# Time and band attention on one core: value banks, shared roots, score order, and 64-key halves for the band scores

## The chip, the cores and the metric

One core of one Trainium2 chip runs the whole program. The metric is device time in microseconds of one execution. The kernel before took 2722.84 us (median of three runs, 2720.51 to 2723.32).

## What is computed

The input is x of shape [2, 256, 128, 128] in fp32: 2 batches, 256 time steps, 128 frequency bins, 128 channels. Three blocks follow each other, each with a layer norm ahead and a residual around it: causal attention over time (4 heads of 32 channels), attention over frequency inside a band of 16 bins to both sides, and a feed-forward block of 512 inner channels with an exact gelu.

```python
xt = _ln(x, ln_t_w, ln_t_b).transpose(0, 2, 1, 3)
x = x + _mha(xt, t_wi, t_bi, t_wo, t_bo, H_T, cm).transpose(0, 2, 1, 3)   # cm: causal
xf = _ln(x, ln_f_w, ln_f_b)
x = x + _mha(xf, f_wi, f_bi, f_wo, f_bo, H_F, bm)                         # bm: |i - j| <= 16
xn = _ln(x, ln_n_w, ln_n_b)
h = jax.nn.gelu(xn @ w1.T + b1, approximate=False)
x = x + (h @ w2.T + b2)
```

## The kernel before

**Groups.** The work is cut into groups of 512 rows of 128 channels (NT = 4 tiles of 128 rows). First come 128 `OverTime` groups: two frequency bins with all 256 time steps each. Then come 16 runs; a run is 8 `OverBands` groups (four time steps with all 128 bins each), followed by 8 `FeedForward` groups on the same rows. The time stage writes its result to DRAM, from where the runs load it.

**One group's way.** VectorE takes mean and variance (`statistics`, L447). The reciprocal root of the variance comes from a pair of ScalarE functions, Ln and Exp (`root_by_scalar`, L462), and three small VectorE steps (`refine`, L474), for the time groups with a PSUM bank as intermediate place (`root_in_bank`, L470). `normalize` (L483) writes the normalized rows, `turn` (L500) transposes them in blocks of 32 and sends them to DRAM, and `fetch` (L512) brings them back with channels on the partitions. TensorE makes queries and keys (`queries_keys`, L576) and values (`values`, L595); ScalarE copies all three from PSUM to SBUF (`take_query`, `take_key`, and `take_values`, L602). TensorE makes the scores, ScalarE their exponentials, GpSimd masks them; `weigh` sums the weights by a product with ones (into `rp`) and weighs the values (into `op`); ScalarE and VectorE invert the sums and divide (`invert`, L607; `divide`, L620: `bank<-bank,r`, then `u`, then `oT`); TensorE makes the output product and VectorE adds it to the residual (`finish`, L641).

**Matmuls by tiles.** All products use a part of the TensorE array. Products with a weight of 32 columns work in tiles of 128 rows by 32 columns. Scores have only 32 channels of a head to sum over: head h lies in row group h. With 64 keys such a product takes one of eight tiles of 32 rows by 64 columns: the row group is the head, the column group the 64-key half. With 128 keys it takes one of four tiles of 32 by 128. In fp32 each product is two passes, and the trace counts each pass.

**Scores over time.** For one group and head there are 8 products with 64 keys each. They are named by kind, head, sequence s and half e, as in `f110`: kind f (`first_scores`, L678) are the keys of the first 128 steps against all later queries (256 queries for half 0, 192 for half 1), kind s (`second_scores`, L685) the keys of the second 128 steps (64 queries for half 0, 128 for half 1). One block holds the s products of group n and the f products of group n+1, 32 in all, in an order written out by hand (`TIME_ORDER`, L738; `time_scores`, L744).

**Scores over bands.** `OverBands.scores` (L764) goes over four tiles of 128 bins. Tiles 0 and 3 are cut in halves of 64 keys, each with the 80 queries that the band reaches; tiles 1 and 2 take 128 keys and 128 queries at once. Head 3's band is applied by VectorE (`bank<-bank,band`), the other three are masked by GpSimd after the exponentials.

**Order of the work.** `run` (L1057) is one loop over n, in which each step of a group is written at the iteration and place where it is to be issued. Every instruction goes through `InOrder.pinned` (L881), which keeps that program order on each engine; so the profile shows L881 for all of them, and groups are told apart by the names of their tiles.

**Banks.** PSUM has eight banks. In the time stage they have names: a0 to a3 take the f scores of heads 0 to 3, b0 to b3 the s scores; `Attention.place` gives the other results a bank that is free at that moment, and after each iteration the names move round in a cycle (end of `run`). In the bands banks are taken in turn. A bank is taken again only after its reader is done; this makes the waits between engines.

**Input.** `load` (inside `groups`, L956 and L988) issues the DMAs for x, twelve groups ahead in the steady state, into a ring of four tiles of four groups each. The very first tile is `k.x0`, loaded at the start.

Of the kernel before, what the change touches and what calls it, by code (L numbers as in the profile page):

```python
# [19 lines left out]
P = 128  # L20
H = 4
D = 32
BAND = 16
# [404 lines left out]
class Group:  # L428
# [17 lines left out]

    def statistics(self):  # L447
        path, vector = self.path, self.path.vector
        self.mv = path.small.tile([P, NT, 2], F32, name="mv", bufs=16)
        stats = path.small.tile([P, NT, 6], F32, name="stats")  # L450
        for i in range(NT):
            vector.bn_stats(stats[:, i, :], self.src()[:, i, :])
        for i in range(NT):
            vector.bn_aggr(self.mv[:, i, :], stats[:, i, :])

    def root(self):
        path, gpsimd = self.path, self.path.gpsimd
# [3 lines left out]

    def root_by_scalar(self, to=None):  # L462

        path = self.path
        ln = path.small.tile([P, NT], F32, name="lnv")
        path.scalar.activation(ln, self.mv[:, :, 1], AF.Ln, bias=path.eps)
        self.root0 = path.small.tile([P, NT], F32, name="root0") if to is None else to
        path.scalar.activation(self.root0, ln, AF.Exp, scale=-0.5)

    def root_in_bank(self):  # L470
        path = self.path
        self.root_by_scalar(path.ps[path.banks["b2"]][:, 0:NT])

    def refine(self):  # L474

        path, vector, y = self.path, self.path.vector, self.root0
        t = path.small.tile([P, NT], F32, name="vy")
        vector.scalar_tensor_tensor(t, self.mv[:, :, 1], EPS, y, ALU.add, ALU.mult)
        vector.scalar_tensor_tensor(t, t, -0.5, y, ALU.mult, ALU.mult)
        self.rstd = path.small.tile([P, NT], F32, name="rstd", bufs=16)  # L480
        vector.scalar_tensor_tensor(self.rstd, t, 1.5, y, ALU.add, ALU.mult)

    def normalize(self):  # L483
# [60 lines left out]
    def values(self):  # L544
        pass
# [17 lines left out]
        pass  # L563


class Attention(Group):
    which = None
    swapped = ()
    place = {}
# [88 lines left out]
class OverTime(Attention):  # L658
# [4 lines left out]
    swapped = (1, 3)  # L663
    early, late = (1, 2), (0, 3)

    def first_tiles(self):
        path = self.path

        self.p0 = path.work.tile([P, 2, H, 2 * P], F32, name="p0", tag="p", bufs=3)
        self.s0 = {h: path.bank([P, 2, 2 * P], "sp", path.banks[f"a{h}"]) for h in range(H)}  # L670
# [65 lines left out]


TIME_ORDER = """  # L738
    s000 s301 s011 s300 f101 f211 s100 s311 s010 s001 s111 f300 f110 f000 f210 f301
    f201 f011 f200 f111 s310 f100 f010 f310 s211 f311 s201 f001 s110 s101 s210 s200  # L740
""".split()


# [14 lines left out]
class OverBands(Attention):  # L758
# [5 lines left out]
    def scores(self, heads):  # L764
        path = self.path
        self.sp = {h: path.bank([P, NT * P], "sp") for h in heads}
        for i, part in ((0, HALF), (1, P), (2, P), (3, HALF)):
            reach = 0 if part == P else BAND
            for e in range(0, P, part):
                a = i * P + (e - reach if e else 0)  # L770
                q, keys = slice(a, a + part + reach), slice(i * P + e, i * P + e + part)
                for h in heads:
                    r = rows_of(h)
                    path.tensor.matmul(
                        self.sp[h][e : e + part, q], self.kT[r, keys], self.qT[r, q], start=True, stop=True
                    )

    def first_function(self):
# [107 lines left out]
class BoundedPath:  # L886
    def __init__(self, ctx, tc, k):
        self.tc, self.nc, self.k = tc, tc.nc, k
        self.xpool = ctx.enter_context(tc.tile_pool(name="xpool", bufs=3))
        self.work = ctx.enter_context(tc.tile_pool(name="work", bufs=3))  # L890
        self.small = ctx.enter_context(tc.tile_pool(name="small", bufs=6))
        ps = ctx.enter_context(tc.tile_pool(name="ps", bufs=1, space=PSUM))
        self.ps = [ps.tile([P, BANK], F32, name=f"bank{i}", tag=f"bank{i}") for i in range(8)]
        self.next_bank = 0
        self.held = {}
        self.banks = dict(zip(("a1", "a2", "b0", "b3", "a0", "a3", "b1", "b2"), range(8)))
        self.tensor, self.vector = InOrder(tc, tc.nc.tensor), InOrder(tc, tc.nc.vector)
        self.scalar, self.gpsimd = InOrder(tc, tc.nc.scalar), InOrder(tc, tc.nc.gpsimd)
        self.sync = InOrder(tc, tc.nc.sync)
        self.dram = ctx.enter_context(tc.tile_pool(name="turns", bufs=3, space=DRAM))  # L900
        self.zero = 0.0
        self.once = once = ctx.enter_context(tc.tile_pool(name="once", bufs=1))
        self.eps = once.tile([P, 1], F32, name="eps")
        tc.nc.vector.memset(self.eps, EPS)

        self.band = once.tile([P, P], F32, name="band")
        tc.nc.gpsimd.memset(self.band, 0.0)
        for s in (1, -1):
            tc.nc.gpsimd.affine_select(
                out=self.band, in_=self.band, compare_op=ALU.is_ge, fill=-1e30, base=BAND,  # L910
                pattern=[[-s, P]], channel_multiplier=s,
            )
# [25 lines left out]
    def quad(self, held, name, bufs):  # L938

        held[name] = self.xpool.tile([P, NT, NT, P], F32, name=name, tag=name, bufs=bufs)  # L940

    @staticmethod
    def longer(quad, i, a):

        return quad.rearrange("p s t c -> p (s t c)")[:, i * P - a : (i + 1) * P + D - a]

    def groups(self, x, out):
# [3 lines left out]
        for b in range(B):  # L951
            for f0 in range(0, FB, GA):
                held = {}


                def load(g, f0=f0, b=b, held=held):  # L956
                    if b == f0 == 0:
                        held["x"] = k.x0
                        return
                    if g == 0:  # L960
                        self.quad(held, "x", 4)
                    f = f0 + g // NC_T * NT
                    self.sync.dma_start(held["x"][rows_of(g)], self.of_times(x[b], g, slice(f, f + NT)))

                def store(g, f0=f0, b=b, held=held):
                    for i in range(NT if g % 2 else 0):
                        f = f0 + i // NC_T * NT + g
                        self.sync.dma_start(
                            self.of_times(k.x1[b], i, slice(f - 1, f + 1)), held["res"][rows_of(i), :, g - 1 : g + 1]
                        )  # L970

                def part(name, g, i=None, a=0, held=held):
                    if name == "res" and name not in held:
                        self.quad(held, "res", 2)
                    if i is not None:
                        return self.longer(held[name], i * NT + g, a)
                    return held[name][:, :, g]

                for g in range(NT):
                    yield OverTime(self, partial(part, "x", g), partial(part, "res", g), partial(load, g), partial(store, g))  # L980
        for b in range(B):
            for r0 in range(0, T, RUN):
                run = []
                for t0 in range(r0, r0 + RUN, GB):
# [2 lines left out]

                    def load(g, t0=t0, b=b, held=held):  # L988
                        if g == 0:
                            self.quad(held, "x", 4)  # L990
                            self.quad(held, "x2", 2 * RUN // GB)
                        self.sync.dma_start(
                            held["x"][rows_of(g)].rearrange("q g t c -> q (g t) c"),
                            self.of_bands(k.x1[b], t0 + NT * g, NT),
                        )
# [61 lines left out]
    def run(self, x, out):  # L1057
# [12 lines left out]
                do(n, *names)  # L1070


        run0 = [i for i in range(len(groups)) if at(i, OverBands)][: RUN // NT]
        due = dict(zip(run0, (-5, -4, -4, -3, -1, 0, 1, 2)))
        due = {n: [i for i in run0 if run0[0] + due[i] == n] for n in range(-12, len(groups) + 2)}
# [3 lines left out]
        for n in range(-12, len(groups) + 2):  # L1079
# [6 lines left out]
            do_at(n + 4, FeedForward, "root")  # L1086
            do(n, "first_half", "first_function", "first_mask")
            if n >= 0:
                do_at(n + 5, OverTime, "statistics")
            if old is not None or new is not None:  # L1090
                time_scores(old, new)
                b = self.banks
                Attention.place = dict(yp=b["b0"], rp=b["b3"], op=b["a1"], qp=b["a2"], kp=b["b1"], vp=b["b2"])
            else:
                Attention.place = {}
            if old is not None:
# [9 lines left out]
            if new is not None:  # L1106
                new.first_weights(new.early[1:])
            if n >= 0:
                do_at(n + 5, OverTime, "root_in_bank")
            if turn:  # L1110
                do(n, "second_half", "second_function")
            do_at(n + 3, OverTime, "fetch")
            do_at(n + 2, (OverBands, FeedForward), "fetch")

            for i in (2 * n + 12, 2 * n + 13) if n < -2 else (n + 10,) if n < 2 else ():
                if i >= NT:
                    do(i, "load")
            if n < -8 or n >= 0:
                do(n + 12, "load")
            if n >= 0:  # L1120
                for i in due[n]:
# [4 lines left out]
                do(n - 2, "finish")  # L1126
            do_at(n + 4, OverTime, "turn")
            if n >= 0:
                do_at(n + 5, OverTime, "refine")
            if n < 0:  # L1130
                do(n + 5, "statistics")
            do_at(n + 5, FeedForward, "statistics")
# [34 lines left out]
            if old is not None or new is not None:  # L1167

                b = self.banks
                self.banks = dict(  # L1170
                    a1=b["b1"], a2=b["a2"], b0=b["a0"], b3=b["a3"], a0=b["b0"], a3=b["b3"], b1=b["a1"], b2=b["b2"]
                )


# [67 lines left out]
```

## Time and profile before

| | |
|---|---|
| time, median of three runs | 2722.84 us (2720.51 to 2723.32) |
| profiled execution | 2717.44 us |
| its span, first to last instruction | 2715.7 us |
| mean granted TensorE clock | 0.998 |
| busy: TensorE / its weight loads | 2687.0 / 1817.2 us |
| busy: VectorE / ScalarE / GpSimd | 2181.6 / 1854.8 / 1947.9 us |
| DMA, mean | 128 GB/s |

In lines of the profile, PE is TensorE's matmuls, PEld its weight loads, DVE VectorE, ACT ScalarE, POOL GpSimd, SP the engine whose queue issues the DMAs. A line of a timeline has the start in us from the start of the span, the length, the engine, the line of code, the operation, out<-in by tile names, partitions by elements, and xN for N instructions of the same kind in a row; brackets give idle time ahead of it and what ended it. In a block of matmuls, the length shown goes to the modelled end of the last one, and the next block may begin before that. PSUM tiles are all called `bank`. Names that help: `qT,kT` are score products, `xnT,wf` queries and keys, `wf,xnT` values, `p,ones` and `p,v` (bands: `pf`) the weighing, `wn,oT` the output product, `xnT,w1f` and `w2T_sb,hT` the feed-forward products.

### The profile page before, as it was taken

What the parts mean: (1) busy time and instruction counts of PE and PEld (TensorE: products, weight loads), DVE (VectorE), ACT (ScalarE), POOL (GpSimd) and SP (SyncE); (2) the same over time, 40 slices, a digit from 0 to 9 for tenths busy, and PEclk for the clock granted to TensorE, in tenths of its full rate; (3) what the DMA queues carried; (4) which work ended last, traced back from release to release, by engine and by line L of the source; (5) the groups of instructions that cost most, each with busy time, mean ns of one, the idle gap of its engine ahead of it and who ended that gap; (6) DMA issues with size and microseconds to landing.
All of it is one profiled execution on the core that took longest, in us unless ns stands there. A gap on an engine that the chain in (4) does not pass through costs nothing.

```text
span 2715.7 us, 152631 instructions
## 1 busy us (share of the span) xinstructions
PE 2687.0 (99%) x66614; PEld 1817.2 (67%) x66614; DVE 2181.6 (80%) x6708; ACT 1854.8 (68%) x3620; POOL 1947.9 (72%) x2297
## 2 busy tenths in 40 slices
PE   8999999999999999999999999999999999999998
PEld 5676776767676666666666666666666666666665
DVE  6888888888888896977868769678687696886874
ACT  6999999999999864564655746646556466465563
POOL 4999999999999885756667657566666575665762
PEclk9999999999999999999999999999999999999999
DMA  5555555555555444445445454454444444544533
GB/s 148 146 152 153 150 150 149 150 147 147 147 159 148 131 113 121 117 112 129 111 117 133 105 125 122 112 131 107 118 129 110 124 118 113 131 108 119 131 92 82
DMA packets 471496, 346.83 MB, mean 128 GB/s; under 512 B 43296, under 2 KB 405152, under 8 KB 470816
## 3 DMA queue, kind: packets, MB, share of 16 engines
q1 hardware_dynamic: 469568, 335.92, 47.2%
q8 instruction: 524, 8.59, 1.4%
q10 hardware_dynamic: 1248, 1.05, 0.2%
q14 instruction: 156, 1.28, 0.2%
HBM read 169.03 MB, written 167.77 MB: 124 GB/s over the span
## 4 chain that ended last, share of the span: by engine, by line
PE 86%; DVE 11%; DMA 1%; issue 0%; ACT 0%; POOL 0%; SPq 0%; DVEq 0%; POOLq 0%; ACTq 0%
PE bank L881 86%; DVE xh L881 2%; DVE bank L881 2%; DVE stats L881 1%; DVE u L881 1%; DVE z L881 1%; DVE x L881 1%; DVE oT L881 1%; DMA xnT<-turned 1%; DVE mv L881 1%; DMA x<-in_x 0%; POOL p L881 0%; POOL pf L881 0%; DMA rows_sb<-in_rows 0%; DMA turned<-z 0%
## 5 line engine op out<-in xcount | busy, mean ns | idle before, releaser
L881 ACT ACTIVATE hT<-bank,b 128x512 f32<-128x512 f32 x512 | 346.7, 687 | 527.3 <-PE bank L881 508.5
L881 POOL TENSOR_SCALAR_AFFINE_SELECT pf<-pf 128x512 f32<-128x512 f32 x768 | 476.8, 635 | 291.0 <-ACT pf L881 264.5
L881 DVE TENSOR_SCALAR xh<-x,mv,rstd 128x160 f32<-128x160 f32 x1536 | 597.0, 431 | 14.3
L881 PEld LDWEIGHTS bank<-w2T_sb,hT 128*32 128x32 f32 x16384 | 457.1, 110 | 63.2 <-issue 39.7
L881 PE MATMUL bank<-xnT,wf 128*32 128x512 f32 x4096 | 488.6, 594 | 3.0 <-ACT p L881 3.0
L881 PE MATMUL bank<-w2T_sb,hT 128*32 128x128 f32 x16384 | 474.3, 273 | 0.2 <-ACT hT L881 0.2
L881 PE MATMUL bank<-xnT,w1f 128*32 128x512 f32 x4096 | 472.7, 592 | 0.0
L881 ACT ACTIVATE p<-bank 128x512 f32<-128x512 f32 (+1 forms) x1024 | 430.5, 495 | 30.6 <-PE bank L881 4.6
L881 POOL TENSOR_SCALAR_AFFINE_SELECT p<-p 128x1024 f32<-128x1024 f32 (+2 forms) x384 | 363.5, 947 | 92.6 <-ACT p L881 84.3
L881 DVE TENSOR_TENSOR res<-bank,res 128x512 f32<-128x512 f32 x256 | 175.8, 687 | 253.8 <-PE bank L881 250.5
L881 PE MATMUL bank<-qT,kT 32*64 32x80 f32 (+5 forms) x14336 | 368.2, 288 | 3.6 <-DVE oT L881 2.2
L881 PEld LDWEIGHTS bank<-qT,kT 32*64 32x64 f32 (+1 forms) x14336 | 300.5, 138 | 84.4 <-ACT kT L881 48.8
L881 PEld LDWEIGHTS bank<-wf,xnT 128*32 128x32 f32 x8192 | 233.1, 110 | 157.6 <-issue 102.8
L881 POOL TENSOR_TENSOR p<-p,p 128x512 f32<-128x512 f32 x256 | 324.1, 1288 | 10.7
L881 ACT ACTIVATE pf<-bank 128x512 f32<-128x512 f32 x512 | 264.5, 603 | 92.5 <-PE bank L881 92.0
L881 DVE BATCH_NORM_STATS2 stats<-x 128x6 f32<-128x128 f32 x1536 | 326.6, 275 | 0.1
L881 PEld LDWEIGHTS bank<-xnT,w1f 128*32 128x32 f32 x4096 | 150.5, 110 | 193.9 <-issue 169.0
L881 DVE STREAM_TRANSPOSE z<-xh 128x512 f32<-128x512 f32 x384 | 272.1, 709 | 9.3
L881 PE MATMUL bank<-wn,oT 128*32 128x128 f32 x8192 | 274.8, 274 | 0.4 <-ACT p L881 0.3
L881 POOL TENSOR_TENSOR rstd<-rstd,mhalf 128x4 f32<-128x4 f32 x248 | 256.6, 1035 | 20.7
L881 PE MATMUL bank<-wf,xnT 128*32 128x128 f32 x8192 | 271.1, 273 | 0.0
L881 POOL TENSOR_SCALAR rstd<-mv 128x4 f32<-128x4 f32 x248 | 56.3, 227 | 296.6 <-DVE mv L881 295.9
(97 smaller groups left out, 3646.1 us busy)
## 6 DMA issues: line engine op xcount, KB each, us to landing
turned<-z SPq DMA_DIRECT2D x1536, 64.0 KB, 2.6
xnT<-turned SPq DMA_DIRECT2D x384, 256.0 KB, 3.0
x<-in_x SPq DMA_DIRECT2D x128, 256.0 KB, 4.2
x<-res SPq DMA_DIRECT2D x256, 128.0 KB, 3.2
x<-x SPq DMA_DIRECT2D x128, 256.0 KB, 4.2
out<-res SPq DMA_DIRECT2D x256, 128.0 KB, 2.5
w1T_sb<-in_w1T ACTq DMA_DIRECT2D x1, 256.0 KB, 6.0
w2T_sb<-in_w2T ACTq DMA_DIRECT2D x1, 256.0 KB, 7.4
```

What stands on the lines that cost most here:

```text
L881: return self.tc.keep_in_program_order(emit(*args, **kwargs))
```

## The change

It has five parts.

1. *Time values in two banks.* `OverTime` gets its own `values` and `take_values`: tiles 0 and 1 go to one bank (`vp0`), tiles 2 and 3 to another (`vp1`), and ScalarE copies each half by itself.
2. *Roots for four groups.* A new class `Four` joins four time groups: their means and variances lie in one tile of 16 columns, and the root pair and the three refining steps run once for the four. The first 12 groups keep the old way. Statistics of a time group are taken eight groups ahead instead of five.
3. *Order and banks.* `TIME_ORDER` names the same 32 products in another order. The cycle of banks is another: now the f scores of head 1 follow in the bank of the row sums `rp`, those of head 0 in that of `op`, those of head 3 in that of the keys `kp`, and the s scores of head 1 in that of `vp0`. In the order of instructions this adds one wait of TensorE per time group, for VectorE's `u`, ahead of `f110`.
4. *Bands by halves.* `OverBands.scores` cuts all four tiles into halves of 64 keys by 80 queries; products with 128 keys are gone. A group has 32 score products in place of 24.
5. *Input.* Each fifth input tile is `k.x0`, so the ring has five; loads are issued fourteen groups ahead.

The diff, cut to its core:

```diff
+class Four(Group):
+    def __init__(self, path, groups):
+        self.path, self.groups = path, groups
+        for group in groups:
+            group.four = self
+
+    def part(self, tile, group):
+        i = self.groups.index(group) * NT
+        return tile[:, i : i + NT]
+
+    def refine(self):
+        super().refine()
+        for group in self.groups:
+            group.rstd = self.part(self.rstd, group)
...
 class OverTime(Attention):
...
+    def means(self):
+        if self.four is None:
+            return super().means()
+        if self is self.four.groups[0]:
+            self.four.mv = self.path.small.tile([P, NT * NT, 2], F32, name="mvs", bufs=3)
+        return self.four.part(self.four.mv, self)
+
+    def values(self):
+        path = self.path
+        wv = path.k.wf[self.which][:, 2 * P : 3 * P]
+        self.vp = [path.bank([P, 2, P], "vp", self.place.get(f"vp{s}")) for s in range(2)]
+        for i in range(NT):
+            product(
+                path, self.vp[i // 2][:, i % 2], self.xnT[:, i * P : (i + 1) * P], wv, turn=2 if i in self.swapped else 0
+            )
+
+    def take_values(self):
+        path = self.path
+        self.v = path.work.tile([P, NT, P], F32, name="v", bufs=4)
+        for s in range(2):
+            path.scalar.copy(self.v[:, 2 * s : 2 * s + 2], self.vp[s])
...
 TIME_ORDER = """
-    s000 s301 s011 s300 f101 f211 s100 s311 s010 s001 s111 f300 f110 f000 f210 f301
-    f201 f011 f200 f111 s310 f100 f010 f310 s211 f311 s201 f001 s110 s101 s210 s200
+    s310 s301 s011 s000 s300 s010 s001 f110 f201 f200 f111 f301 f101 f310 f000 f211
+    f210 f100 f001 s111 f010 s311 s201 f300 f311 s211 f011 s100 s210 s101 s110 s200
 """.split()
...
     def scores(self, heads):
         path = self.path
         self.sp = {h: path.bank([P, NT * P], "sp") for h in heads}
-        for i, part in ((0, HALF), (1, P), (2, P), (3, HALF)):
-            reach = 0 if part == P else BAND
-            for e in range(0, P, part):
-                a = i * P + (e - reach if e else 0)
-                q, keys = slice(a, a + part + reach), slice(i * P + e, i * P + e + part)
+        for i in range(NT):
+            for e in range(2):
+                keys = slice(e * HALF, (e + 1) * HALF)
+                a = i * P + e * (HALF - BAND)
+                q = slice(a, a + HALF + BAND)
                 for h in heads:
                     r = rows_of(h)
                     path.tensor.matmul(
-                        self.sp[h][e : e + part, q], self.kT[r, keys], self.qT[r, q], start=True, stop=True
+                        self.sp[h][keys, q], self.kT[r, i * P + e * HALF : i * P + (e + 1) * HALF], self.qT[r, q],
+                        start=True, stop=True,
                     )
...
+    def input_quad(self, held):
+
+        self.inputs += 1
+        if self.inputs % 5 == 0:
+            held["x"] = self.k.x0
+        else:
+            self.quad(held, "x", 4)
...
             if n >= 0:
-                do_at(n + 5, OverTime, "statistics")
+                if n + 5 < 3 * NT:
+                    do(n + 5, "statistics")
+                if n >= NT:
+                    do_at(n + 2 * NT, OverTime, "statistics")
...
-                Attention.place = dict(yp=b["b0"], rp=b["b3"], op=b["a1"], qp=b["a2"], kp=b["b1"], vp=b["b2"])
+                Attention.place = dict(yp=b["b0"], rp=b["b3"], op=b["a1"], qp=b["a2"], kp=b["b1"], vp0=b["b0"], vp1=b["b2"])
...
-            for i in (2 * n + 12, 2 * n + 13) if n < -2 else (n + 10,) if n < 2 else ():
+            for i in (2 * n + 12, 2 * n + 13) if n < 2 else (n + 14,):
                 if i >= NT:
                     do(i, "load")
-            if n < -8 or n >= 0:
+            if n < -8:
                 do(n + 12, "load")
...
                 self.banks = dict(
-                    a1=b["b1"], a2=b["a2"], b0=b["a0"], b3=b["a3"], a0=b["b0"], a3=b["b3"], b1=b["a1"], b2=b["b2"]
+                    a1=b["b3"], a2=b["a2"], b0=b["a0"], b3=b["a3"], a0=b["a1"], a3=b["b1"], b1=b["b0"], b2=b["b2"]
                 )
```

Where `root_in_bank` and `refine` of a time group stood in `run`, they are now called for the first 12 groups one by one and after that for the four whose last group it is.

More of the change, by code (lines that the diff above doesn't have):

```diff
@@ L448, in statistics @@
         path, vector = self.path, self.path.vector
-        self.mv = path.small.tile([P, NT, 2], F32, name="mv", bufs=16)
+        self.mv = self.means()
         stats = path.small.tile([P, NT, 6], F32, name="stats")
@@ L454, in statistics @@
             vector.bn_aggr(self.mv[:, i, :], stats[:, i, :])
+    def means(self):
+        return self.path.small.tile([P, NT, 2], F32, name="mv", bufs=16)
     def root(self):
@@ L462, in root_by_scalar @@
     def root_by_scalar(self, to=None):
-        path = self.path
-        ln = path.small.tile([P, NT], F32, name="lnv")
+        path, n = self.path, self.mv.shape[1]
+        ln = path.small.tile([P, n], F32, name=f"lnv{n}")
         path.scalar.activation(ln, self.mv[:, :, 1], AF.Ln, bias=path.eps)
-        self.root0 = path.small.tile([P, NT], F32, name="root0") if to is None else to
+        self.root0 = path.small.tile([P, n], F32, name="root0") if to is None else to
         path.scalar.activation(self.root0, ln, AF.Exp, scale=-0.5)
@@ L471, in root_in_bank @@
         path = self.path
-        self.root_by_scalar(path.ps[path.banks["b2"]][:, 0:NT])
+        self.root_by_scalar(path.ps[path.banks["b2"]][:, 0 : self.mv.shape[1]])
     def refine(self):
-        path, vector, y = self.path, self.path.vector, self.root0
-        t = path.small.tile([P, NT], F32, name="vy")
+        path, vector, y, n = self.path, self.path.vector, self.root0, self.mv.shape[1]
+        t = path.small.tile([P, n], F32, name=f"vy{n}")
         vector.scalar_tensor_tensor(t, self.mv[:, :, 1], EPS, y, ALU.add, ALU.mult)
         vector.scalar_tensor_tensor(t, t, -0.5, y, ALU.mult, ALU.mult)
-        self.rstd = path.small.tile([P, NT], F32, name="rstd", bufs=16)
+        self.rstd = path.small.tile([P, n], F32, name="rstd" if n == NT else "rstds", bufs=16 if n == NT else 3)
         vector.scalar_tensor_tensor(self.rstd, t, 1.5, y, ALU.add, ALU.mult)
@@ L563, in finish @@
         pass
+class Four(Group):
[10 more added lines that the diff above has]
+            group.rstd = self.part(self.rstd, group)
 class Attention(Group):
+    four = None
     which = None
@@ L664, with means @@
     early, late = (1, 2), (0, 3)
+    def means(self):
+        if self.four is None:
[16 more added lines that the diff above has]
+            path.scalar.copy(self.v[:, 2 * s : 2 * s + 2], self.vp[s])
     def first_tiles(self):
@@ L894, in __init__ @@
         self.next_bank = 0
+        self.inputs = 0
         self.held = {}
@@ L960, in load @@
                     if g == 0:
-                        self.quad(held, "x", 4)
+                        self.input_quad(held)
                     f = f0 + g // NC_T * NT
@@ L989, in load @@
                         if g == 0:
-                            self.quad(held, "x", 4)
+                            self.input_quad(held)
                             self.quad(held, "x2", 2 * RUN // GB)
@@ L1070, in do_at @@
                 do(n, *names)
+        timed = [g for g in groups if isinstance(g, OverTime)]
+        fours = {i + NT - 1: Four(self, timed[i : i + NT]) for i in range(3 * NT, len(timed), NT)}
         run0 = [i for i in range(len(groups)) if at(i, OverBands)][: RUN // NT]
@@ L1108, in run @@
             if n >= 0:
-                do_at(n + 5, OverTime, "root_in_bank")
+                if n + 5 < 3 * NT:
+                    do(n + 5, "root_in_bank")
+                if n + 2 * NT in fours:
+                    fours[n + 2 * NT].root_in_bank()
             if turn:
@@ L1128, in run @@
             if n >= 0:
-                do_at(n + 5, OverTime, "refine")
+                if n + 5 < 3 * NT:
+                    do(n + 5, "refine")
+                if n + 2 * NT in fours:
+                    fours[n + 2 * NT].refine()
             if n < 0:
```

## The prediction

> **What bounds the kernel now.** I read the page first: the busy times, and the chain that ended last.
>
> ```profile
> PE 2687.0 (99%) x66614; PEld 1817.2 (67%) x66614; DVE 2181.6 (80%) x6708; ACT 1854.8 (68%) x3620; POOL 1947.9 (72%) x2297
> ...
> PE 86%; DVE 11%; DMA 1%; issue 0%; ACT 0%; POOL 0%; SPq 0%; DVEq 0%; POOLq 0%; ACTq 0%
> ```
>
> TensorE is busy for 99%, with 11% of the chain on VectorE. So the second view is the busy time by stage: the time stage (300 to 900 us), then two iterations of the band half of one run, the first bands and the later ones, then the feed-forward half.
>
> ```profile
> 300.00:900.00 600.00, 599.98 (x16084) 420.20 (x16080) 524.86 (x1676) 544.72 (x1256) 548.84 (x502) 1.00 0.55 150
> 1086.31:1092.94 6.63, 6.63 (x176) 4.33 (x171) 5.42 (x10) 5.01 (x10) 3.69 (x7) 1.00 0.35 89
> 1092.94:1099.58 6.64, 6.64 (x176) 4.34 (x172) 6.49 (x18) 5.05 (x10) 4.96 (x9) 1.00 0.24 54
> 1138.85:1173.48 34.63, 34.63 (x809) 23.76 (x804) 22.35 (x82) 13.74 (x20) 24.55 (x27) 1.00 0.60 151
> ```
>
> After the length come the busy times of PE, PEld, DVE, ACT and POOL. In the time stage the next engine (POOL) has 8.5% left, so TensorE alone sets the pace. In the later band iterations VectorE has 6.49 of 6.64 us: two engines are full at once. The timelines show one group's blocks on TensorE, first of the time stage, then of the bands:
>
> ```profile
> 904.50 1.48 PE L881 MATMUL bank<-qT,kT 32*64 32x64 f32 x64
> 905.91 1.08 PE L881 MATMUL bank<-wn,oT 128*32 128x128 f32 x32
> ...
> 1102.29 1.38 PE L881 MATMUL bank<-qT,kT 32*64 32x80 f32 x48
> 1103.59 1.07 PE L881 MATMUL bank<-pf,ones 128*32 128x512 f32 x8
> ```
>
> From one block's start to the next, the scores take 1.404 us in the time stage (exact records; 1.41 above) and 1.305 in the bands. The periods are 7.168 us per time group (median of 112) and 6.638 per band group.
>
> **What the Trainium skill says.**
> 1. "TensorE: Matmul & The Clock Gate", Part 3, "Packing small matmuls — row/col tiling": products on different tiles of the array run at once, some 4 ns apart, but start and end strictly in program order. The trace agrees on the overlap (6.7 ns between passes on different tiles) and not on the order: in the block above a product on a free tile starts before an earlier one whose tile is still busy. The measurement decides.
> 2. "TensorEngine Tiling (Array Packing)", "Key Properties": a change of tiling mode drains TensorE. It agrees: about 90 ns lie between the end of the last score product and the start of the next block, and the first product on each tile comes 51 ns after that tile's load.
> 3. "PSUM — Partial Sum Buffer", "PSUM bank collisions raise a hardware error": guard by bank, not by address. The kernel's waits do so: scores of head 2 wait until the whole value copy has left their bank (copy ends .722 us into the block, first such product at .775).
>
> **The change, part by part.**
>
> *Bands by 64-key halves.* Now tiles 0 and 3 go as halves (64 keys by 80 queries), tiles 1 and 2 with 128 keys: the mode changes from 64 to 128 columns and back inside each block. The records split it into .326 + .657 + .326 = 1.305 us (rounded). A 64-column stretch is 51 (first load) + 2 passes × 69 on each tile + 47 (last start offset) + 90 (drain) = 326 ns. After the change the block is one stretch: each of 8 tiles gets 4 products of 2 passes, 8 passes × 69.3 + 51 + 47 + 90 = 742 ns. That removes .563 us of TensorE per band group; over 128 groups it would be 72 us. That eight tiles keep up such a beat over many passes is seen in the time stage, where passes of 64 columns follow each other by 57.5 ns on one tile.
>
> But VectorE doesn't allow all of it. Its timeline in the same run:
>
> ```profile
> 1090.69 0.70 DVE L881 SCALAR_TENSOR_TENSOR bank<-bank,band 128x512 f32<-128x512 f32 x1 [1.07 <-PE bank L881]
> ...
> 1097.33 0.70 DVE L881 SCALAR_TENSOR_TENSOR bank<-bank,band 128x512 f32<-128x512 f32 x1
> ...
> 1101.24 0.66 DVE L881 TENSOR_TENSOR x<-bank,x 128x512 f32<-128x512 f32 x1
> ...
> 1102.54 0.69 DVE L881 SCALAR_TENSOR_TENSOR u<-bank,r 128x512 f32<-128x512 f32 x1
> ...
> 1103.94 0.70 DVE L881 SCALAR_TENSOR_TENSOR bank<-bank,band 128x512 f32<-128x512 f32 x1
> ```
>
> Up to the fourth band of a run VectorE waits for TensorE (the bracket; the idle times of the bands of this run are 4.14, 3.32, .15, .51 and 1.07 us). From the band correction at 1090.69 on, feed-forward statistics lie in each iteration (10 instructions become 18 or 19) and it works without a wait: 1097.33 to 1103.94 is 6.61 us, with no bracket. So the last four bands keep a period of about 6.61 whatever TensorE saves. TensorE will wait where it depends on VectorE: the band scores of head 2 take the bank that the x addition (1101.24 to 1101.90) frees, .39 us before 1102.29; weighing the last band (1123.23) waits for u of the band before, which ends at 1123.08. Only the four score blocks ahead of the stretch count: 4 × .565 = 2.26, with small waits before the stretch 2.28 us per run. Fifteen runs × 2.28 = 34.2; run 0, whose first bands follow the time stage with VectorE late, I put at half, 1.1. Sum **35.3 us**. Bounds: 33 (one block in eight runs lost) to 72 (VectorE's stretch not rigid). POOL's masks have 1.04 us of room in the third band, .47 after; ACT is at 5.05 of 6.64. Both hide.
>
> *Order of the time scores.* All 64 passes go to 8 tiles (head = row, 64-key half = column); each tile has 640 columns in two passes, 1.09 us of work (passes of 64, 128, 192 and 256 columns follow each other by 57.5, 109, 163 and 216 ns on one tile). So the block ends 1.09 us after the tile that starts last, plus .09 of drain. In the old order the tile of head 2, half 0 is first named at place 15 and starts .222 us into the block: ends 1.314, next block at 1.404, as recorded. In the new order the last is head 1, half 1, at place 11; with the same rules (6.7 ns between starts[...]) it starts at .154 and ends at 1.242. Saving **.072 us** per group, bounds 0 and .13 (every tile started in the first 8 places). About 126 groups: 9.0 us, 0 to 16.
>
> *Values in two banks.* One ACT copy 128x512 (585 ns) becomes two of 128x256; I take 391 ns each from the exponentials of that size. The key copy before them ends .14 us ahead of the block (903.77 + .59 against 904.50), so the first bank is free at about .21 us into the block, the second at about .6 instead of .72. Neither holds the new order: it names head 1's product of the second kind (first bank) at place 20 and head 2's (second bank) at place 23, and going through the order by the same rules, the latter wait moves the end only if the bank comes free after about .75. ACT pays 2 × .391 − .585 = +.20 us. Cost on the path: nothing, covered by ACT's 9% of room. Its worth is that the new order has no stall.
>
> *Roots for four groups.* The pair of 0.33 and 0.18 us on ACT and three small VectorE steps (.44 together) run once per four groups: −.38 us on ACT and −.33 on VectorE per time group, both off the path: nothing.
>
> *Cycle of banks.* New first scores of head 1 take the bank of the old row sums, so TensorE waits for u before them (125 waits are added). u ends .92 us before the block starts (902.89 + .69 against 904.50), so it costs nothing; queued behind it would be the rest of the block and everything after. Loads go out two groups earlier into five buffers in place of four: SP has no wait that ends late, so nothing. From time stage to bands (933 to 966 us) TensorE waits for VectorE, with blocks up to 2.83 us; of this I expect ±3 us.
>
> Sum: 35.3 + 9.0 = **44.3 us**. The profiled execution took 2717.44 (span 2715.7 and 1.7 around it), so 2673.1; the median of the runs shown is 2722.84, 5.4 us more (0.2%), so **2678.5**.
>
> **Rivals.**
> - *VectorE is no wall* (.12): all eight blocks count, 72 + 9 = 81, 2642. For it: TensorE has no gap in any iteration now. Against: no idle bracket on VectorE from 1090.69 on, and a work order that is fixed.
> - *The time stage gives nothing* (.18), because ACT's exponentials, now later behind two copies, hold the next output product, or starts are held by program order as the skill has it: 2722.8 − 35.3 = 2687.5. Against: exp of head 0 starts at .783 and the product could go at 1.22.
> - *Weight loads set the beat of the halves* (.08): PEld's mean is 110 ns for a load of 32 columns; if a round of eight tiles takes 107 ns, the block is 51 + 856 + 47 + 90 = 1.044, saving .26: four blocks in 16 runs 16.6, with 9.0: 2697. Against: 57.5 ns per round in the time stage.
> - *Slower: the added wait for u* (.04). It stands ahead of the eighth product of the time block (about .05 us in). If u comes later than .97 us after its present place, each group waits for the excess: from .36 us of excess it outweighs the 44 us (126 × .36 = 45). At .8 it is 101 − 44 = +57, 2779. For it: VectorE has 12.5% idle only and idles mainly before u's chain, for ACT. Against: the change takes work from both.
>
> **Numbers.** The forecast has .55, the rivals .12, .18, .08, .04; .03 is left for what I don't see. The forecast's own bounds, 2667 to 2690, with the third case take in 2667 to 2697 for .81 of the chance; towards the first rival VectorE may yield in part, so the range is 2656 to 2699. About 0.2% (5.4 us) is what a measurement can tell from no change: faster .94, within .02, slower .04.
>
> **What would show it.** A band score block of about .74 us in place of 1.305; in the last four bands of a run waits of TensorE for VectorE of some .5 us each, VectorE without a pause; a run 2.3 us shorter (before 109.1). A time period of 7.10 us with a score block of 1.33. If run periods fall by 4 us or more, the wall was none; if blocks are .74 and runs are not shorter, the stretch begins earlier than I read. If the time period stays at 7.17, the tile rule is wrong.

## The result, and the profile after

The changed kernel takes **2685.45 us** (median of four runs, 2683.14 to 2690.14) against 2721.68 for the kernel before on the same chip: a ratio of 0.987, with an interval of 0.9853 to 0.9887. That is 36 us less; the prediction said 44.3 less, 2678.5, in a range of 2656 to 2699.

The page of the changed kernel, busy times and the chain that ended last:

```profile
PE 2638.5 (98%) x68662; PEld 1805.6 (67%) x68662; DVE 2146.5 (80%) x6447; ACT 1844.5 (69%) x3574; POOL 1950.0 (73%) x2297
...
PE 80%; DVE 15%; DMA 2%; issue 1%; ACT 1%; SPq 0%; DVEq 0%; ACTq 0%
```

TensorE's busy time fell by 48 us, more than the kernel gained; VectorE's share of the chain rose from 11% to 15% and DMA's from 1% to 2%. TensorE waits now where it did not before. The timeline of TensorE in the time stage, and in two later bands of a run with the end of that run's bands:

```profile
412.82 1.39 PE L926 MATMUL bank<-qT,kT 32*64 32x64 f32 x64
414.14 1.08 PE L926 MATMUL bank<-wn,oT 128*32 128x128 f32 x32
...
1087.74 1.12 PE L926 MATMUL bank<-qT,kT 32*64 32x80 f32 x64
1088.79 1.06 PE L926 MATMUL bank<-pf,ones 128*32 128x512 f32 x8
...
1094.12 1.07 PE L926 MATMUL bank<-qT,kT 32*64 32x80 f32 x64
1095.12 1.06 PE L926 MATMUL bank<-pf,ones 128*32 128x512 f32 x8
...
1110.48 3.62 PE L926 MATMUL bank<-xnT,w1f 128*32 128x512 f32 x32
1114.83 1.06 PE L926 MATMUL bank<-pf,ones 128*32 128x512 f32 x8 [0.74 <-DVE u L926]
```

Start to start, the time scores take 1.32 us (1.316 in the single records; 1.404 before). The band scores take 1.05 and 1.00 (median 0.995 over the profile; 1.305 before), where 0.742 was forecast. The last line is the wait for `u` that the prediction named: the last band of a run is weighed only when VectorE has finished with the band before. The two feed-forward products ahead of it take 3.43 us together where nothing waits; here 4.35 us lie between their start and the weighing, in the kernel before 3.74:

```profile
1119.49 3.62 PE L881 MATMUL bank<-xnT,w1f 128*32 128x512 f32 x32
1123.23 1.07 PE L881 MATMUL bank<-pf,ones 128*32 128x512 f32 x8
```

VectorE in the same run, from the correction of the fourth band on:

```profile
1082.69 0.70 DVE L926 SCALAR_TENSOR_TENSOR bank<-bank,band 128x512 f32<-128x512 f32 x1 [0.76 <-PE bank L926]
...
1089.23 0.69 DVE L926 SCALAR_TENSOR_TENSOR bank<-bank,band 128x512 f32<-128x512 f32 x1
...
1095.76 0.69 DVE L926 SCALAR_TENSOR_TENSOR bank<-bank,band 128x512 f32<-128x512 f32 x1
```

The last wait for TensorE is 0.76 us long; after that a loop takes 6.53 us (1089.23 to 1095.76), while TensorE's own iterations are 6.33 to 6.38. A run takes 107.34 us in the median (109.12 before).

Last, the waits of TensorE in the time stage (60 to 925 us), with total, times and longest in us:

```profile
PE bank L926 <- DMA xnT<-turned: 2.4, 1, 2.4
PE bank L926 <- issue: 0.2, 1, 0.2
```

The kernel before has no such line there. Once in this execution the transposed rows came late; with what followed from it, that group's period is 11.42 us instead of 7.08.

So the profiled execution's span, 34.3 us shorter, divides thus: 5.0 by the 122nd time group (0.5 in the first four groups, then 118 x 0.088 = 10.4, less 5.9 by which single groups were longer than their usual period more than before), 1.7 from there to the end of run 0, and 27.6 in the fifteen other runs, 1.84 each.

### The profile page after: what moved, and what is told of

Read it like the earlier page. It is cut to its first block, busy times and chain, and to the rows that moved or that the text cites. A ratio compares the mean times of both kernels' runs of the same rounds, so it can differ in the third digit from the quotient of the medians.

```text
span 2681.4 us, 156498 instructions
## 1 busy us (share of the span) xinstructions
PE 2638.5 (98%) x68662; PEld 1805.6 (67%) x68662; DVE 2146.5 (80%) x6447; ACT 1844.5 (69%) x3574; POOL 1950.0 (73%) x2297
## 3 DMA queue, kind: packets, MB, share of 16 engines
q10 hardware_dynamic: 1248, 1.05, 0.2%
## 4 chain that ended last, share of the span: by engine, by line
PE 80%; DVE 15%; DMA 2%; issue 1%; ACT 1%; SPq 0%; DVEq 0%; ACTq 0%
PE bank L926 80%; DVE xh L926 4%; DVE bank L926 3%; DVE stats L926 2%; DVE z L926 2%; DVE u L926 2%; DVE x L926 1%; DMA xnT<-turned 1%; DVE mv L926 1%; DMA turned<-z 1%; SPq L926 0%; DVE oT L926 0%; ACT p L926 0%; DVE vy L926 0%; DMA f_wiT_sb<-in_f_wiT 0%
## 5 line engine op out<-in xcount | busy, mean ns | idle before, releaser
L926 DVE TENSOR_SCALAR xh<-x,mv,rstd 128x160 f32<-128x160 f32 x1072 | 417.7, 431 | 10.0
L926 PE MATMUL bank<-qT,kT 32*64 32x80 f32 (+4 forms) x16384 | 317.3, 273 | 5.2 <-DVE u L926 1.8
L926 PEld LDWEIGHTS bank<-qT,kT 32*64 32x64 f32 x16384 | 273.4, 131 | 58.3 <-ACT kT L926 47.4
```

Of the source, the lines that this page charges most:

```text
L926: return self.tc.keep_in_program_order(emit(*args, **kwargs))
```

## The experiments

Two theories stood after the result. **Theory**: the band scores by halves are held by something that was not in the sum, which lets 32 passes go at the pace of the tiles and slows the rest; VectorE sets the end of the bands; the time part brings its 0.088 us per group and loses some of it to late rows. **Rivals**: the slower blocks come from the other parts of the change, or from the tiles themselves; VectorE is no wall.

e1 to e4 ran on one chip, e5 to e8 on a second, e9 to e12 on a third; each ratio is against the runs of the kernel before on the same chip.

### One part alone: e1 and e2

e1 is the kernel before with this edit alone; e2 is the changed kernel with the reverse of it:

```diff
-        for i, part in ((0, HALF), (1, P), (2, P), (3, HALF)):
+        for i in range(NT):
+            for e in range(2):
...
```

> The kernel before with the band scores by halves alone. Theory (first 32 passes of a block come at the pace of the tiles, the other 32 at that of the supply of instructions; VectorE then sets the end of the bands): score blocks of about 0.99 us, runs of 107.3 us, time period 7.168, total 2721.7 - 29 = 2693. Rival (the slower blocks come from the new cycle of banks or from the roots, not from the halves themselves): blocks of 0.74, runs of 106.8, total 2686.

Measured: 2693.42 us (before: 2722.57), ratio 0.990 (0.9885 to 0.9914). Blocks of 0.995 in the median, runs of 107.29, time period 7.168. All as the theory has it. The slow blocks come with the halves alone; banks and roots have no part in them.

> The changed kernel with the old band scores. Theory (the time part is worth 0.088 us per group, less some waits for DMAs): time period 7.08, runs of 109.1, total 2721.7 - 7 = 2715, between -11 and -3. Rival (what the shorter period brings is lost to late loads of the transposed rows): within 2 us of before.

Measured: 2715.26 us (2708.93 to 2724.45, nine runs), ratio 0.9965 (0.995 to 0.9981); time period 7.08, runs of 109.1. The two parts, 29.2 and 7.3 us, add up to the 36 of the whole change. The time part could have brought 126 x 0.088 = 11.1. Its profile, of the slowest of the nine runs, shows where such an execution loses it:

```profile
PE bank L925 <- DMA xnT<-turned: 7.6, 7, 2.2
PE bank L925 <- issue: 0.7, 2, 0.4
```

### Inside the time part: e3 and e4

```diff
 TIME_ORDER = """
-    s310 s301 s011 s000 s300 s010 s001 f110 f201 f200 f111 f301 f101 f310 f000 f211
+    s000 s301 s011 s300 f101 f211 s100 s311 s010 s001 s111 f300 f110 f000 f210 f301
...
```

> The changed kernel with the old order of the time scores. Theory (the order alone shortens the block): time period 7.168, total 2685.5 + 11 = 2696. Rival (the shorter block comes from the banks that are free earlier): period stays near 7.08, total 2686.

Measured: 2700.48 us, ratio 0.9922 (0.9909 to 0.9934); period 7.216 to 7.237, block 1.471. The rival falls: without the new order the other parts bring nothing here. But the theory is off too: the old order is 0.067 us slower among the new banks than in its own (1.404). The single records show where. The old order names `s100` as its seventh product, and in the new cycle the s scores of head 1 lie in the bank of the first value half. So `s100` now waits until ScalarE has copied that half: the copy ends 0.124 us into the block and the product starts at 0.176 (medians; in the kernel before it starts at 0.040), and what stands behind it is late with it. The new order names its first s product of head 1 as the twentieth, and none of its blocks shows a wait for a value copy.

e4 puts the values back in one bank with one copy (`vp=b["b2"]`, and without the new `values` and `take_values`).

> The changed kernel with the time values in one bank and one copy. Theory (the new order needs head 2's bank only at places 23 to 32, and the old copy frees it at 0.72 us, just before that matters): time period 7.08 to 7.10, total 2685 to 2688. Rival (without the split the new order stalls on the copy): period 7.15 or more, total 2694 or more.

Measured: 2691.62 us, ratio 0.9884 (0.9866 to 0.9902). The period is 7.117, between the two: the block is 1.353, so the split is worth 0.037 us per group, some 4.7 us over 126 groups by the periods (the totals, with their intervals, don't separate it). The forecast that the copy's end at 0.72 us comes just in time was wrong by that much: in the single records `s201`, the first s product of head 2, starts 0.754 us into the block in the changed kernel and 0.775 here, 52 ns after the copy's end (0.723); and its second pass then follows after 160 ns, where it takes 109 in the changed kernel.

### The wall in the bands: e5, e6, e7

e5 leaves out VectorE's correction of head 3; e6 gives head 3 to GpSimd (`by_vector = 0`).

> The changed kernel without VectorE's band correction of head 3 (that head's weights are left unmasked in the bands: work left out). Theory (VectorE sets the end of the bands; TensorE waits 0.9 us for it ahead of the last weighing of a run): that wait falls to about 0.1, runs fall from 107.35 by 0.6 to 0.9 us, total 2685.5 - 12 = 2673. Rival (TensorE alone sets the pace of the bands, the wait only moves): runs of 107.2 or more, total 2684 or more.

Measured: 2660.43 us, ratio 0.9786 (0.9769 to 0.9802), with 2717.24 for the kernel before on this chip. Runs fall to 106.23, by 1.1 us, more than forecast, and no wait for VectorE is left. Waits of TensorE from 1069 to 2650 us, first the kernel before, then the changed kernel, then e5:

```profile
PE bank L881 <- DVE u L881: 1.2, 5, 0.5
```

```profile
PE bank L926 <- DVE u L926: 10.7, 15, 0.8
PE bank L926 <- issue: 0.3, 1, 0.3
```

```profile
PE bank L921 <- issue: 0.5, 1, 0.5
```

Fifteen waits, one per run, of 0.7 us each, are gone. VectorE is the wall; the rival falls. (Leaving the correction out also shortens the way from the scores of head 3 to their exponential; e11 below keeps it there, at half the width, and all of these waits but 0.2 us go as well.)

> The changed kernel with head 3's band masked by GpSimd like the other three, instead of VectorE. Theory (VectorE is the wall; GpSimd takes 2 x 0.635 us more per band, 4.98 + 1.27 = 6.25 of a 6.33 us iteration): runs shorter by 0.4 to 0.9 us, total 2673 to 2679. Rival (GpSimd, now full, becomes the wall): TensorE waits for masks, runs of 108 or more, total 2695 or more.

Measured: 2688.18 us, ratio 0.9888 (0.9871 to 0.9904), runs of 107.73. No wait for VectorE is left here either, yet nothing is won. In the third and the last band of each run the sum of weights now waits for the last mask: the eighth pass of the product with ones starts over a microsecond after its block, 0.51 us after that mask's end (1399.94 in the lines here).

```profile
1399.39 1.21 PE L926 MATMUL bank<-pf,ones 128*32 128x512 f32 x7
1400.28 0.40 PE L926 MATMUL bank<-pf,v 128*32 128x128 f32 x6
1400.44 0.59 PE L926 MATMUL bank<-pf,ones 128*32 128x512 f32 x1
```

That is the rival's mechanism, at a smaller price than it gave: GpSimd takes the wall's place where it is late already.

e7 keeps the 32 products and gives each 128 queries:

```diff
-                a = i * P + e * (HALF - BAND)
-                q = slice(a, a + HALF + BAND)
+                q = slice(i * P, (i + 1) * P)
```

> The changed kernel with 128 queries in each band score product instead of 80 (the added scores are masked anyway). A tile then takes 109 ns per pass instead of 69. Theory (the second half of a block is held by the supply of passes, about 16 ns each or 130 ns per round of eight): the block grows only to about 51 + 8 x 109 + 47 + 90 = 1.06 us, or 1.1 with the knee smeared, runs of 107.6, total 2689. Rival (the 0.25 us over 0.742 are a loss on the tiles themselves, so the added work comes on top): block of 0.99 + 8 x 0.040 = 1.31, runs of 108.6 or more, total 2705.

Measured: 2692.1 us, ratio 0.9904 (0.9887 to 0.992), runs of 108.13, block 1.19 (1.136 at least), between the two forecasts. The timeline:

```profile
1398.45 1.28 PE L925 MATMUL bank<-qT,kT 32*64 32x128 f32 x64
1399.67 1.07 PE L925 MATMUL bank<-pf,ones 128*32 128x512 f32 x8
```

The single records of the blocks without a wait decide it. The table gives the time from the first start of a block to that of the 32nd pass, and from there to the 64th (median, and the least; by the choice of blocks the median for 80 queries lies between 0.51 and 0.53).

| | first 32 passes | next 32 passes | at the pace of the tiles |
|---|---|---|---|
| 80 queries (changed kernel) | 0.305 us | 0.52 (0.433) | 4 x 0.069 = 0.277 |
| 128 queries (e7) | 0.425 us | 0.565 (0.513) | 4 x 0.109 = 0.436 |

The first 32 passes go exactly at the pace of the tiles in both. The next 32 lose 0.24 us with short products, 0.13 with long ones: with 0.16 us more work on each tile they take only 0.05 us longer. So this is no loss that comes on top, but a pace of about 16 to 18 ns per pass under both (0.52 and 0.565 us for 32). It is a mean, not a hard limit: single blocks of the changed kernel took from 0.433 to 0.584 us. My forecast of 1.06 used the tiles' pace for the second half too; 0.425 + 32 x 0.016 + 0.2 for the last product and the drain gives 1.14.

### Where the slow half comes from: e10

The Trainium skill ("PSUM — Partial Sum Buffer", "Engine vs sequencer instructions") speaks of a 64-deep queue of TensorE. 32 passes, each a weight load and a product, are 64 instructions, as many as the fast part of a block has. If they stand ready when the block begins and later ones are supplied more slowly, long passes in between should let the queue fill again:

```diff
         for i in range(NT):
+            if i == 2 and self.ahead is not None:
+                self.ahead.sums()
```

(`sums` is the product with ones of the band before, taken out of its `weigh`.)

> The changed kernel with the product with ones of the previous band (8 passes of 512 columns) put between the 32nd and the 33rd pass of the band scores. Theory (32 passes stand ready in TensorE's queue, later ones come at 16 ns each; during the long passes the queue fills again): both stretches run at the pace of the tiles, 0.305 us from the first start to the last, 0.46 us each with the drain, sum 0.93 instead of 0.99 though one mode change is added; total within 6 us of the changed kernel. Rival (the later products are slow in themselves): the second stretch still takes 0.52 us, sum 1.14.

Measured: both stretches as the theory has it, start to start 0.46 us, and 0.305 from first start to last:

```profile
1188.82 0.53 PE L935 MATMUL bank<-qT,kT 32*64 32x80 f32 x32
1189.28 1.06 PE L935 MATMUL bank<-pf,ones 128*32 128x512 f32 x8
1190.28 0.53 PE L935 MATMUL bank<-qT,kT 32*64 32x80 f32 x32
1190.74 1.08 PE L935 MATMUL bank<-pf,v 128*32 128x128 f32 x32
```

The same products that took 0.52 us now take 0.305. What is slow is not the products but their coming after 32 others. In the changed kernel there is a second sign: 12 band blocks are held after their fourth pass by a wait, and in 10 of these (waits of 0.05 to 0.9 us) the fast part is just four passes longer than in the others. It ends the same number of passes after the hold, however long the hold was. No change of the tiling mode lies there, so it is not such a change that makes the passes fast again. The total missed its forecast by far: 2751.18 us, ratio 1.0108 (1.008 to 1.0137), runs of 111.24. VectorE's correction now waits for the second stretch (0.31 us in each loop), and TensorE's first stretch then waits for VectorE's x addition (0.89 us in place of 0.46): the product with ones lies inside the loop of the two engines.

```profile
1208.45 0.96 PE L935 MATMUL bank<-qT,kT 32*64 32x80 f32 x32
1209.34 1.07 PE L935 MATMUL bank<-pf,ones 128*32 128x512 f32 x8
...
1211.19 0.70 DVE L935 SCALAR_TENSOR_TENSOR bank<-bank,band 128x512 f32<-128x512 f32 x1 [0.31 <-PE bank L935]
```

All this fits a stock of 32 passes that runs dry, as the theory has it; the trace has no view of the queue, and what limits the supply was not found.

### Late rows, and a better version: e8, e9, e11, e12

e8 is the changed kernel with the loads as before (four buffers, twelve groups ahead); e9 is the changed kernel once more; e11 splits head 3's band between VectorE (tiles 0 and 1) and GpSimd (2 and 3); e12 is e11 with the loads of e8.

```diff
-            sp = self.sp[h].rearrange("p (i q) -> p i q", i=NT)
+            sp = self.sp[h].rearrange("p (i q) -> p i q", i=NT)[:, 0:2]
...
-        for h in range(H - self.by_vector):
-            blk = self.p[:, h]
+        for h in range(H):
+            n = NT if h < H - self.by_vector else 2
+            blk = self.p[:, h, NT - n :]
```

> The changed kernel with the input loads as before (four buffers, twelve groups ahead). Theory (the waits for late transposed rows come from the shorter time period and the shifted steps, not from the earlier loads): total 2683 to 2690, rows still late in some places. Rival (the moved loads push the rows' transfers): no waits for rows in the time stage, total 2680 or less.

Measured: 2681.05 us, ratio 0.9865 (0.9849 to 0.9882). The total lies between the two forecasts, and the ratio is that of the changed kernel (0.987); no wait for rows in the time stage, as the rival says.

> The changed kernel once more, on the chip of the three other runs of this call, as their measure. Both theories: 0.987 of before, between 0.985 and 0.989.

Measured: 2692.33 us (2679.43 to 2701.43), before 2724.56, ratio 0.9895 (0.9872 to 0.9918), just outside the forecast.

> The changed kernel with head 3's band split: VectorE corrects tiles 0 and 1, GpSimd masks tiles 2 and 3. VectorE's loop falls from 6.53 to about 6.2 us, under TensorE's 6.33; GpSimd rises from 5.0 to about 5.7. Theory (VectorE is the wall and GpSimd at 5.7 is none): runs of 106.3 to 106.6 instead of 107.35, total 0.9 us x 16 = 14 us under the changed kernel. Rival (masks become late as in the run with the whole band on GpSimd): runs of 107.4 or more, total the same or above.

Measured: 2680.77 us, ratio 0.9837 (0.9812 to 0.9863), runs of 106.74. VectorE is relieved and GpSimd is no wall: 0.6 us per run less than the changed kernel (107.34), a little less than forecast (106.6 at most). The total is 11.6 us under e9 on the same chip, where 14 were forecast.

> The split band with the input loads as before (four buffers, twelve groups ahead). Theory (the earlier loads make the transposed rows late in the time stage, which costs 3 to 5 us): that much under the run with the split band alone, and no rows that land within 0.2 us of their use. Rival (the late rows come from the shorter period): equal within 2 us, rows late here too.

Measured: **2670.86 us**, ratio 0.9812 (0.9787 to 0.9836), the best of the versions that compute all. Its interval lies clear of that of e9 on the same chip. Against e11 the medians differ by 10 us where 3 to 5 were forecast, but the intervals overlap.

On the late rows: of the ten profiled executions with the earlier loads, eight show TensorE waiting for rows in the time stage, in all from 0.8 to 7.6 us; e6 and e9 show none. Of the four with the old loads (before, e1, e8, e12) none does, though e8 and e12 have the shorter period. That speaks for the loads as the cause; but no two totals on one chip separate it beyond their intervals, and e8 gained no more against the kernel before than the changed kernel did. So it stays likely, not shown.

## Why the prediction held, and where its sum was off

- *Bands: mechanism right, one term wrong.* Predicted 35.3 us, measured 29.2 alone (e1). The step of the sum that failed is "8 passes x 69.3 + 51 + 47 + 90 = 742 ns". It carried the pace of two rounds, and the time stage's 57.5 ns between passes on one tile, over to eight short rounds in a row. But the time stage's 64 passes take 1.15 us from the first start to the last, 18 ns per pass, so it never asked for a faster supply than 16 ns. The block came to 0.995: 0.31 us saved, not 0.563. (One reading in it was also wrong, without weight in the sum: the first product does not come 51 ns after its tile's load. In the records it starts within 2 ns of the load's start, and the second pass on a tile follows 120 ns after the first instead of 69; the 51 ns lie there.)
- *VectorE's wall: right, and it hid half of that error.* Without the wall the error would have been 128 x 0.25 = 32 us. Only the blocks ahead of VectorE's stretch count: 4 x 0.31 = 1.24 us per run (the fourth correction comes 1.34 us sooner after the run's start, 20.32 instead of 21.66 in the median). The measured 1.8 has a second piece that the prediction denied: it took VectorE's 6.61 us loop as free of waits. The loop without TensorE is 6.53: in the kernel before, the correction starts 0.71 us after the start of `oT`, in the changed one 0.61. So it was TensorE that set the pace of the later bands before (6.64 us for both engines), and a wait of about 0.1 us, too short for a bracket, was given back in each of four loops: 0.47 us per run (32.47 to 32.00 from that correction to the end of the last `u`).
- *In part luck.* These two errors lie on opposite sides: the block's 0.25 us too little makes 4 x 0.25 x 16 = 16 us too much saving in the sum, and the freed waits that it put at nothing bring 0.47 x 15 = 7 us. Without this second one the total would have come out some 15 us off the forecast, in place of 8.
- *Where the wait would appear: half right.* The wait at the last weighing is there (0.74 us in its bracket); waits of some 0.5 us in each of the last four bands are mostly not, since TensorE's blocks were slower and its iterations took 6.33 us by themselves. The 0.2 us by which VectorE's loop is longer add up over four loops to some 0.8, close to what TensorE waits at the end; only the last score block of the run is longer by a wait.
- *Order of the time scores: right, a little small.* 0.072 forecast, 0.088 measured; the rule of the tile that starts last gave 1.332 us, the trace 1.316. That tile (head 1, half 1) does end last, but its start was misjudged: the sum has it at 0.154 us, the records at 0.067, which is 0.118 with the 51 ns of a first load; 23 ns of that were lost again, where its last pass comes late. So two misses partly cancel in the 1.332. e3 shows that the gain needs the new order, and that the old one in the new banks loses.
- *Values in two banks.* "The new order has no stall" is right with two banks; that one bank would bind only from 0.75 us on was wrong by 0.037 us per group (e4).
- *Loads, "SP has no wait that ends late, so nothing":* not confirmed. The time part alone brought 7.3 us (e2) where its shorter blocks give 11.1. Waits for rows are what the profiles show in their place; that the loads cause them is likely only.
- *Wait for `u`, roots:* costs of nothing, as forecast: 111 groups from 100 to 890 us have a median block of 1.316, and the trace lists no wait of TensorE for `u` in the time stage.
- *Rivals.* "VectorE is no wall" is refuted by e5. "Weight loads set the beat" came near in size (0.26 against 0.31 saved per block) for another reason: load and product of a tile keep their pace as long as instructions stand ready (e10).

## What to carry to other kernels

Price a stretch of short products by how many come in a row, not by one round: here the 33rd pass and later cost about 16 ns each, though their tiles were free. When two engines are both full, a saving on one counts only ahead of the stretch in which the other is full, and each relief (e5, e6, e11) should be read from the wait that takes its place. An engine without brackets in its timeline may still wait some 0.1 us per loop; compare the same pair of starts in two places before calling it full.

## What was not expected of the hardware

- Of 64 band score passes on eight tiles, the first 32 start within 0.305 us and the next 32 take 0.43 to 0.58 us; after eight passes of 512 columns (1.0 us) the next 32 are fast again (e10).
- The profiles of several time-stage variants have short stops of TensorE put down to "issue" (0.2 to 1.7 us in all per execution), in which it waits for nothing that the trace names.
- Order and banks are coupled: the same old order took 1.404 us in its own cycle of banks and 1.471 in the new one, where a product that it names early waits for a value copy.
